# Turning the tables and the rows of a macaron S4D block by DMA transposes that read SBUF, without the copy in DRAM, and from the 16th group on

## The chip, the cores and the metric

The program runs on one core of one Trainium2 chip. The metric is the device time of one execution in microseconds; of the kernel before, three runs are given, and one further execution was profiled. Engines are named as the profile names them: PE (matrix products), PEld (its weight loads), DVE, ACT and POOL (the three engines for elementwise work) and SP, which only issues DMAs here.

## The reference

`x` has the shape (8, 2048, 256): 8 sequences, 2048 positions, 256 channels, float32. The output is

```python
x = x + 0.5 * ffn(layernorm(x))
x = x + attn(layernorm(x))       # an S4D convolution, then a layernorm
x = x + 0.5 * ffn(layernorm(x))

ffn(x)  = relu(x @ w1 + b1) @ w2 + b2            # 256 -> 1024 -> 256
attn(x) = layernorm(x + conv(x, K) + x * D) * ln_w + ln_b
K[h, l] = 2 * real(sum_n Ct[h, n] * exp(dtA[h, n] * l))     # 64 states n per channel h
```

The convolution is causal over all 2048 positions, one kernel `K` for each channel.

## The kernel before, in words

The work has three stages. **Stage a** is the first feed-forward sublayer, **the middle** is the S4D layer, **stage b** is the second feed-forward sublayer.

*The sublayers.* The 16384 tokens are cut into 64 groups of 256 (two sequences at 128 positions). The hidden width of 1024 is cut into eight slots of 128. In a slot, `up` (L848) makes six matmuls of 256 columns into a PSUM tile `ph` (a float32 product is made of three products of high and low parts, and there are two halves of the 256 channels), ACT takes the relu and DVE the low part (L926, L927: `hx`), and three slots later (`LAG`) `down` (L859) makes six matmuls into `po`. There are four `ph` banks and four `hx` buffers. PE needs the normalized tokens with the channels on the partitions: `xh` and `xl`, the high and low part of the transposed `xn`. They come in one of two ways, chosen in `ffn_in` (L752):

- *by PE*: four 128x128 transposes into `pt` (L794), then ACT's `xh` (L803) and DVE's `xl` (L805);
- *by DMA* (`turn_by_dma`, L810): DVE and ACT split `xn` into its two planes of 16-bit halves (`pl`, L815), SP writes them to a DRAM tile `xp` (L819), three slots later SP issues a DMA transpose from `xp` into `pt` (L823), three slots after that DVE and ACT put the halves together again (`xf`, L833, in an order fixed by hand), ACT makes `xh` (L835) and DVE `xl` (L837).

Stage a turns groups 0 to 43 by PE and 44 to 63 by DMA (`DMA_A = 44`), stage b groups 0 and 1 by PE and the rest by DMA (`DMA_B = 2`). `pre_a` and `pre_b` start the work on a group 18 or 19 slots before its first matmul.

*The tables P.* Beside stage a runs a background generator, `matrices` (L258): it makes, for every pair of channels (2 channels x 64 states on 128 partitions) the powers of the state's factor at 128 positions, real and imaginary. In 32 batches of four pairs, 128x1024 numbers each, `make` (L587) computes a batch on POOL into a room of `u` (there are four rooms, so batch n waits until batch n-4 has left), `spread` (L613) has ACT split it into planes of 16-bit halves (L620), SP writes these to DRAM (`pv`, L623) and the batch itself to `o_dram` (L625); `turn` (L628) issues a DMA transpose from `pv` back over `planes` (L631); `transpose` (L639) has DVE and ACT put the halves together in the batch's room (L646, order fixed by hand) and SP writes it to `pt_dram` (L650). There are two `planes` buffers, used in turn, and a batch goes through four steps of six sub-steps each (`BACK = 3`).

*What sets the order.* Each slot of stage a adds 1.32 to a clock; the generator names a price for each sub-step (9.1 or 10.3 for a batch, `PA` and `PB_`), and `fill` (L898) lets it run until it has caught up. Two marks are due: "half" at group 32 (the first 16 batches lie in a part of `u` that the output of groups 32 to 47 needs) and "tables" at group 48; what is missing then is emitted at once. SP, ACT and DVE run their instructions in the order of the program; the order itself is made by a scheduler, except where `keep_in_program_order` fixes it. All DMAs named here are issued by SP, except the loads `xa` (L981) and the stores `x_dram` (L999), which ACT issues.

*The middle* reads `pt_dram` and `o_dram`, runs the scan over 16 chunks on DVE and makes the outputs with PE. Nothing of it is changed.

Of the kernel before, what the change touches and what calls it, by code (L numbers as in the profile page):

```python
# [13 lines left out]
U16 = mybir.dt.uint16  # L14
# [5 lines left out]
P = 128  # L20
# [23 lines left out]
def macaron_s4d_kernel(  # L44
# [17 lines left out]
    nc = tc.nc  # L62
    V = nc.vector
    A_ = nc.scalar
# [3 lines left out]
    N = c_re.shape[1]  # L68
# [5 lines left out]
    NDC = H // P  # L74
    NFC = W // P
    NTB = 2
# [8 lines left out]
    PINT = 1  # L85
# [7 lines left out]
    BCH = 8  # L93
    NBT = H // BCH
# [6 lines left out]
    dram = ctx.enter_context(tc.tile_pool(name="dram", bufs=1, space=DRAM))  # L101
    ps = ctx.enter_context(tc.tile_pool(name="ps", bufs=2, space=PSUM))
    upool = ctx.enter_context(tc.tile_pool(name="upool", bufs=1))
    wpool = ctx.enter_context(tc.tile_pool(name="wpool", bufs=1))
# [4 lines left out]
    def bank(tag, name):  # L109
        return ps.tile([P, 512], F32, name=name, tag=tag, bufs=BANKS[tag])  # L110

    def slot(tag, shape, name, dtype=F32):
        return work.tile(shape, dtype, name=name, tag=tag, bufs=BUFS[tag])
# [99 lines left out]


    o_dram = [dram.tile([P, BCH * P], F32, name=f"o_{i}") for i in range(NBT)]
    pv_dram = [dram.tile([P, 2 * BCH * P], U16, name=f"pv_{i}") for i in range(2)]
    pt_dram = [dram.tile([P, BCH * P], F32, name=f"pt_{i}") for i in range(NBT)]
    kpad = dram.tile([H, KROW], F32, name="kpad")

# [38 lines left out]
    def matrices():  # L258
# [24 lines left out]
        for i, src in enumerate(raw + [dtx]):  # L283
            pt = bank("b", f"ptr{i}")
# [22 lines left out]
        r = zim  # L307
# [24 lines left out]
        f, a = r, z  # L332
# [133 lines left out]
        for i in range(H // P):  # L466
            nc.gpsimd.dma_start(
                out=kpad[i * P : (i + 1) * P, P + 1 :], in_=zeros[:, 0 : P - 1]
# [6 lines left out]
        with nc.allow_non_contiguous_dma(reason="256 numbers"):  # L475
            nc.gpsimd.dma_start(
                out=kpad.rearrange("(g c) k -> c g k", c=2)[:, :, P], in_=k0
# [100 lines left out]
        def p_of(bt):  # L578

            r, i = (room[2], 28 + bt % 4 * 8) if bt < first else (room[3], (16, 24, 48, 56)[bt % 4])  # L580
            return r[:, i * P : (i + 8) * P]
# [5 lines left out]
        def make(bt):  # L587

            E = G_
            pp = p_of(bt).rearrange("p (r g k) -> p r g k", r=2, g=PB)  # L590
            tm = tmp_of(bt)
            gs = slice(bt * PB, (bt + 1) * PB)
            br, bi = (
                pb[:, ri, gs, ::-1].unsqueeze(2).to_broadcast([P, PB, NA, NB]) for ri in range(2)
            )
            ar, ai = (
                pa[:, ri, gs, ::-1].unsqueeze(3).to_broadcast([P, PB, NA, NB]) for ri in range(2)
            )
            pr, pi = (pp[:, ri].rearrange("p g (a b) -> p g a b", b=NB) for ri in range(2))
            E.tensor_mul(pr, br, ar)  # L600
            yield
            E.tensor_mul(tm, bi, ai)
            yield
            E.tensor_sub(pr, pr, tm)
            yield
            E.tensor_mul(pi, br, ai)
            yield
            E.tensor_mul(tm, bi, ar)
            yield
            E.tensor_add(pi, pi, tm)  # L610
            yield

        def spread(bt):  # L613

            pl = planes[:, bt % 2]
            pu = p_of(bt).bitcast(U16).rearrange("p (m w) -> p w m", w=2)
            for _ in range(DI):
                yield
            for w in range(2):
                tc.keep_in_program_order(A_.copy(pl[:, w], pu[:, w]))  # L620
                yield
            via = pv_dram[bt % 2]
            nc.sync.dma_start(out=via, in_=pl.rearrange("p w m -> p (w m)"))  # L623
            yield
            nc.sync.dma_start(out=o_dram[bt], in_=p_of(bt))  # L625
            yield

        def turn(bt):  # L628
            for _ in range(PX):
                yield  # L630
            ins = nc.sync.dma_start(  # L631
                out=planes[:, bt % 2].rearrange("p w (k n) -> p (w k) n", n=P),
                in_=pv_dram[bt % 2], transpose=True,
            )
            if PINT:
                tc.keep_in_program_order(ins)
            yield

        def transpose(bt):  # L639
            pl, ptb = planes[:, bt % 2], p_of(bt)  # L640
            for _ in range(PY):
                yield
            pu = ptb.bitcast(U16).rearrange("p (c l r n w) -> p w r l c n", c=2, r=2, n=N, w=2)
            plv = pl.rearrange("p w (r l c n) -> p w r l c n", r=2, c=2, n=N)
            for w in range(2):
                ins = P_REINT[w](pu[:, w], plv[:, w])  # L646
                if PPIN:
                    tc.keep_in_program_order(ins)
            yield
            nc.sync.dma_start(out=pt_dram[bt], in_=ptb)  # L650
            yield

        planes = wpool.tile([P, 2, 2, BCH * P], U16, name="planes", tag="wE")
        P_REINT = (V.tensor_copy, A_.copy)
        PY = 0
        BACK = 3
        DI = 2
        PX = 2
        PA = 9.1
        PB_ = 10.3  # L660
        PPIN = 1

        beside = lags()
        for bt in range(NBT + BACK):
            parts = []
            if 0 <= bt - BACK < NBT:
                parts.append(transpose(bt - BACK))
            if 0 <= bt - 2 < NBT:
                parts.append(turn(bt - 2))
            if 0 <= bt - 1 < NBT:  # L670
                parts.append(spread(bt - 1))
            if bt < NBT:
                parts.append(make(bt))
            for n in range(6):
                for p in parts:
                    next(p, None)
                next(beside, None)
                yield (PA if bt < first + BACK else PB_) / 6
            if bt == first + BACK - 1:
                yield "half"  # L680
# [71 lines left out]
    def ffn_in(xt, name, on_act=NTB, by_dma=False, joint=None):  # L752
# [36 lines left out]
        if by_dma:  # L789
            return (yield from turn_by_dma(xn, name, Y2 - 1 if joint else Y2))  # L790
# [14 lines left out]
        V.tensor_sub(xl, ptv, xh.bitcast(F32))  # L805
        return xh, xl

    xp_dram = [dram.tile([P, 2 * NDC * NTB * P], U16, name=f"xp_{i}") for i in range(4)]

    def turn_by_dma(xn, name, y2):  # L810

        pl = slot("pl", [P, 2, NDC, NTB, P], f"pl_{name}", U16)
        xu = xn.bitcast(U16).rearrange("p i (d c w) -> p d i c w", d=NDC, w=2)
        for w, copy in DEINT:
            copy(pl[:, w], xu[:, :, :, :, w])  # L815
        yield
        via = xp_dram[turned_[0] % 4]
        turned_[0] += 1
        nc.sync.dma_start(out=via, in_=pl.rearrange("p w d i c -> p (w d i c)"))  # L819
        for _ in range(Y1):  # L820
            yield
        pt = slot("pl", [P, 2, NDC * NTB * P], f"pt_{name}", U16)
        nc.sync.dma_start(  # L823
            out=pt.rearrange("p w (k t) -> p (w k) t", t=P), in_=via, transpose=True
        )
        for _ in range(y2):
            yield
        xh = slot("xh", [P, NDC, TOK], f"xh_{name}", F32R)
        xl = slot("xl", [P, NDC, TOK], f"xl_{name}", F32R)
        xf = slot(XF, [P, NDC, TOK], f"xf_{name}")  # L830
        xv = xf.bitcast(U16).rearrange("p d (t w) -> p (d t) w", w=2)
        for w, copy in REINT:
            tc.keep_in_program_order(copy(xv[:, :, w], pt[:, w]))  # L833
        yield
        A_.copy(xh, xf)  # L835
        yield
        V.tensor_sub(xl, xf, xh.bitcast(F32))  # L837
        return xh, xl

    Y1, Y2 = 3, 3  # L840
    XF = "pl"
    DEINT = (0, V.tensor_copy), (1, A_.copy)
    REINT = (0, V.tensor_copy), (1, A_.copy)
    DMA_A = 44
    DMA_B = 2
    turned_ = [0]

    def up(wt, xT, ph, fc):  # L848
        xh, xl = xT
# [126 lines left out]
    def pre_a(g):  # L976
        by_dma = g >= DMA_A
        for _ in range(XL if g < JG else 0):
            yield
        xt = xts[g] = slot("x", [P, NTB, H], f"xa_{g}")  # L980
        ins = (nc.scalar if g >= JG else nc.sync).dma_start(out=xt, in_=hbm(x, g))  # L981
        if g >= JG:
            tc.keep_in_program_order(ins)
        for _ in range(XY):
            yield
        if g >= JG:
            joints[g - JG] = Joint(g - JG, by_dma)
        return (yield from ffn_in(xt, f"a{g}", NTB, by_dma, joints.get(g - JG)))
# [246 lines left out]
    def begin():  # L1235
        for _ in range(sizes[1] // PB):
            next(head)

    sublayer(
        w1t, w2t, pre_a, post_a, 18, "a", load_weights(), chain(matrices(), early()),  # L1240
        {"half": NG // 2, "tables": NG * 3 // 4},
        {NG * SLOTS - 6: lambda: next(head), NG * SLOTS - 1: begin},
# [127 lines left out]
```

## Time and profile before

| | |
|---|---|
| three runs | 1762.26, 1764.35, 1765.85 us; median 1764.35 |
| the profiled execution, its own time | 1761.45 us |
| its span in the trace | 1759.6 us |
| stage a, the middle, stage b (from the chain of work and the first and last products) | about 0 to 800, 800 to 1010, 1010 to 1760 us |
| DVE, ACT, POOL busy, share of the span | 78%, 56%, 33% |
| bytes moved by DMA | 242.68 MB, of them 206.36 MB from SP's queue |

A span is the time between the first and the last instruction that the trace shows; the execution's own time has 1.85 us more around it. A row of a view names the line, the engine, the operation, what is written and read, the count and times. In the views of waits, "A <- B" means that engine A stood idle and B's event ended that. Matmuls overlap in PE's pipeline, so the duration of one (270 to 290 ns) is longer than the distance at which they follow one another.

### The profile page before, as it was taken

To read this page: it belongs to the slowest core of one execution; us is meant where nothing else is said; L and a number is where in the kernel's file an instruction comes from. 1 tells how busy PE (TensorE), PEld (TensorE's weight loads), DVE (VectorE), ACT (ScalarE), POOL (GpSimd) and SP (SyncE) were. 2 spreads that over 40 slices of the span, in tenths; PEclk is the share of its full clock that TensorE was granted. 3 is DMA by queue.
4 is the path that set the end of the run, shared out by engine and by line. 5 is a ranking of instruction groups with operands and counts; after the bars stand their busy time and mean duration, and the time that the engine had idled before them with its cause. 6 is when DMAs were issued, how large, how long until landed. Compare 5 with 4: busy or idle time off the path is not lost.

```text
span 1759.6 us, 40994 instructions
## 1 busy us (share of the span) xinstructions
PE 1724.2 (98%) x15367; PEld 1697.3 (96%) x15367; DVE 1373.7 (78%) x4405; ACT 986.3 (56%) x2178; POOL 588.7 (33%) x550
## 2 busy tenths in 40 slices
PE   9999999989999999999999799999999999999998
PEld 7999999989999999999999799999999999999998
DVE  6998877767776667766999788888888888888884
ACT  4555467667777755544555445555555555555553
POOL 1117989875775115111000122222222222222220
PEclk9999999999999999999999999999999999999999
DMA  5111177669768633246888913333333333333331
GB/s 189 49 37 52 48 214 227 215 185 269 246 218 243 167 101 99 91 111 197 265 261 261 277 55 91 97 91 95 89 94 91 95 92 95 86 97 91 95 92 49
DMA packets 293277, 242.68 MB, mean 138 GB/s; under 512 B 164564, under 2 KB 237012, under 8 KB 292566
## 3 DMA queue, kind: packets, MB, share of 16 engines
q1 hardware_dynamic: 265648, 206.36, 41.1%
q10 hardware_dynamic: 26502, 32.52, 5.4%
q8 instruction: 120, 1.97, 0.4%
q0 software_dynamic: 928, 1.19, 0.3%
q14 instruction: 79, 0.65, 0.1%
HBM read 91.89 MB, written 109.84 MB: 115 GB/s over the span
## 4 chain that ended last, share of the span: by engine, by line
PE 64%; DVE 10%; DMA 3%; issue 1%; ACT 1%; POOL 0%; SPq 0%; ACTq 0%; DVEq 0%; POOLq 0%
PE ph_b L854 21%; PE po_b L864 21%; PE po_a L864 10%; PE ph_a L854 10%; DVE e L1127 2%; DVE te L1128 2%; DMA planes<-pv 1%; DVE xsB L1130 1%; DVE xsA L1130 1%; DVE xsA L1129 1%; DVE xsB L1129 1%; PE py L1172 1%; DVE xsE L1130 0%; DMA pt_a<-xp 0%; DMA xp<-pl_a 0%
## 5 line engine op out<-in xcount | busy, mean ns | idle before, releaser
L864 PE MATMUL po_a<-wa,hx_a 128*128 128x256 f32 x3072 | 456.7, 285 | 11.4 <-DVE hx_a L116 11.2
L854 PE MATMUL ph_a<-xh_a,wa 128*128 128x256 f32 x2048 | 457.0, 287 | 0.8 <-ACT xh_a L803 0.7
L854 PE MATMUL ph_b<-xh_b,wb 128*128 128x256 f32 x2048 | 442.8, 284 | 0.7 <-ACT xh_b L803 0.7
L864 PE MATMUL po_b<-wb,hx_b 128*128 128x256 f32 x3072 | 441.4, 283 | 2.0 <-DVE hx_b L116 2.0
L864 PEld LDWEIGHTS po_a<-wa,hx_a 128*128 128x128 f32 x3072 | 407.2, 192 | 13.8 <-DVE hx_a L116 13.1
L864 PEld LDWEIGHTS po_b<-wb,hx_b 128*128 128x128 f32 x3072 | 400.5, 192 | 2.4 <-DVE hx_b L116 2.4
L854 PEld LDWEIGHTS ph_a<-xh_a,wa 128*128 128x128 f32 x2048 | 356.4, 193 | 3.6 <-ACT wa L194 1.5
L854 PEld LDWEIGHTS ph_b<-xh_b,wb 128*128 128x128 f32 x2048 | 353.0, 193 | 1.1 <-ACT xh_b L803 1.1
L926 ACT ACTIVATE hx_b<-ph_b 128x256 fp32r<-128x256 f32 x512 | 192.0, 381 | 241.5 <-PE ph_b L854 222.9
L926 ACT ACTIVATE hx_a<-ph_a 128x256 fp32r<-128x256 f32 x512 | 194.9, 387 | 236.0 <-PE ph_a L854 222.0
L116 DVE SCALAR_TENSOR_TENSOR hx_a<-ph_a,hx_a 128x256 fp32r<-128x256 f32 x512 | 209.8, 414 | 125.5 <-ACT hx_a L926 123.2
L854 PE MATMUL ph_a<-xl_a,wa 128*128 128x256 f32 x1024 | 290.7, 285 | 0.0
L854 PE MATMUL ph_b<-xl_b,wb 128*128 128x256 f32 x1024 | 285.3, 284 | 0.0
L1305 POOL TENSOR_TENSOR xb<-xb,lnb_sb 128x512 f32<-128x512 f32 x64 | 82.6, 1292 | 504.8 <-DMA xb<-x_dram 342.4
L116 DVE SCALAR_TENSOR_TENSOR hx_b<-ph_b,hx_b 128x256 fp32r<-128x256 f32 x512 | 210.3, 414 | 52.3 <-ACT hx_b L926 46.3
L854 PEld LDWEIGHTS ph_a<-xl_a,wa 128*128 128x128 f32 x1024 | 198.0, 193 | 0.8 <-DVE xl_a L805 0.4
L854 PEld LDWEIGHTS ph_b<-xl_b,wb 128*128 128x128 f32 x1024 | 197.7, 193 | 0.0
L777 POOL TENSOR_TENSOR xa<-xa,hb 128x512 f32<-128x512 f32 x64 | 88.6, 1384 | 282.2 <-ACT xn L730 252.0
L777 POOL TENSOR_TENSOR xb<-xb,hb 128x512 f32<-128x512 f32 x64 | 95.1, 1486 | 55.2 <-ACT xn L730 23.5
L730 ACT ACTIVATE xn<-xb,nb_fb,t_fb 128x255 f32<-128x255 f32 x127 | 69.5, 594 | 76.4 <-DVE nb_fb L116 76.4
L815 DVE COPY pl_b<-xn 128x512 uint16<-128x512 uint16 x62 | 44.5, 717 | 73.3 <-ACT xn L730 73.3
L730 ACT ACTIVATE u<-xa,nb_u,t_u 128x256 f32<-128x256 f32 x104 | 90.1, 866 | 0.0
(263 smaller groups left out, 2511.9 us busy)
## 6 DMA issues: line engine op xcount, KB each, us to landing
o<-u SPq DMA_DIRECT2D x32, 512.0 KB, 3.4
pv<-planes SPq DMA_DIRECT2D x32, 512.0 KB, 3.6
pt<-u SPq DMA_DIRECT2D x32, 512.0 KB, 3.7
tz<-kpad SPq DMA_DIRECT2D x64, 256.0 KB, 4.7
xb<-x_dram SPq DMA_DIRECT2D x64, 256.0 KB, 2.7
out_dram<-xb SPq DMA_DIRECT2D x64, 256.0 KB, 2.9
x_dram<-xa ACTq DMA_DIRECT2D x62, 256.0 KB, 2.0
xp<-pl_b SPq DMA_DIRECT2D x62, 256.0 KB, 2.0
```

The source lines that it names most:

```text
L116: return V.scalar_tensor_tensor(out=o, in0=a, scalar=s, in1=b, op0=op0, op1=op1)
L730: ins = A_.activation(dst, src, AF.Identity, bias=nb[:, i : i + 1], scale=rs[:, i : i + 1])
L777: return G_.tensor_add(xt, xt, hb2.unsqueeze(1).to_broadcast([P, NTB, H]))
L815: copy(pl[:, w], xu[:, :, :, :, w])
L854: nc.tensor.matmul(ph, wt[wp][:, dc, fs], xp[:, dc, :], start=(n == 0), stop=(n == 3 * NDC - 1))
L864: nc.tensor.matmul(po[:, i, :], hp[:, tsl], wt[wp][:, fc, :], start=(fc == 0 and i == 0 and n == 0), stop=(fc == NFC - 1 and n == 2), skip ...
L926: last[A_] = A_.activation(hh, ph, AF.Relu)
L1127: E.tensor_mul(t1, xv[:, :, :, j, :], wr_b)
L1128: E.tensor_mul(t2, xv[:, ::-1, :, j, :], wi_b)
L1129: E.tensor_add(xv[:, :, :, j + 1, :], xv[:, :, :, j + 1, :], t1)
L1130: E.tensor_add(xv[:, :, :, j + 1, :], xv[:, :, :, j + 1, :], t2)
L1305: G_.tensor_add(xt, xt, lnb_sb.unsqueeze(1).to_broadcast([P, NTB, H]))
```

## The change

The DRAM tiles `pv` and `xp` go. The DMA transposes read the planes where they lie in SBUF. For P the two `planes` buffers become one for the planes and one, `turned`, for the transposed planes; a batch goes through three steps (`BACK = 2`), ACT's two copies of a batch, SP's transpose and the putting together have an order fixed by hand, and the putting together starts at the fifth sub-step. For the rows, six slots lie between the issue of the transpose and the putting together, as the two times three did. `DMA_A` goes from 44 to 16, so groups 16 to 43 of stage a change from PE to DMA. Stage b keeps its choice.

```diff
     o_dram = [dram.tile([P, BCH * P], F32, name=f"o_{i}") for i in range(NBT)]
-    pv_dram = [dram.tile([P, 2 * BCH * P], U16, name=f"pv_{i}") for i in range(2)]
...
         def spread(bt):
 
-            pl = planes[:, bt % 2]
             pu = p_of(bt).bitcast(U16).rearrange("p (m w) -> p w m", w=2)
-            for _ in range(DI):
+            yield
+            yield
+            for w in range(2):
+                tc.keep_in_program_order(A_.copy(planes[:, w], pu[:, w]))
                 yield
-            for w in range(2):
-                tc.keep_in_program_order(A_.copy(pl[:, w], pu[:, w]))
-                yield
-            via = pv_dram[bt % 2]
-            nc.sync.dma_start(out=via, in_=pl.rearrange("p w m -> p (w m)"))
+            tc.keep_in_program_order(nc.sync.dma_start(
+                out=turned.rearrange("p w (k n) -> p (w k) n", n=P),
+                in_=planes.rearrange("p w m -> p (w m)"), transpose=True,
+            ))
             yield
             nc.sync.dma_start(out=o_dram[bt], in_=p_of(bt))
             yield
 
-        def turn(bt):
-            for _ in range(PX):
-                yield
-            ins = nc.sync.dma_start(
-                out=planes[:, bt % 2].rearrange("p w (k n) -> p (w k) n", n=P),
-                in_=pv_dram[bt % 2], transpose=True,
-            )
-            if PINT:
-                tc.keep_in_program_order(ins)
-            yield
-
         def transpose(bt):
-            pl, ptb = planes[:, bt % 2], p_of(bt)
-            for _ in range(PY):
+            ptb = p_of(bt)
+            for _ in range(4):
                 yield
             pu = ptb.bitcast(U16).rearrange("p (c l r n w) -> p w r l c n", c=2, r=2, n=N, w=2)
-            plv = pl.rearrange("p w (r l c n) -> p w r l c n", r=2, c=2, n=N)
+            plv = turned.rearrange("p w (r l c n) -> p w r l c n", r=2, c=2, n=N)
             for w in range(2):
-                ins = P_REINT[w](pu[:, w], plv[:, w])
-                if PPIN:
-                    tc.keep_in_program_order(ins)
+                tc.keep_in_program_order(P_REINT[w](pu[:, w], plv[:, w]))
             yield
             nc.sync.dma_start(out=pt_dram[bt], in_=ptb)
             yield
 
-        planes = wpool.tile([P, 2, 2, BCH * P], U16, name="planes", tag="wE")
+        both = wpool.tile([P, 2, 2, BCH * P], U16, name="planes", tag="wE")
+        planes, turned = both[:, 0], both[:, 1]
         P_REINT = (V.tensor_copy, A_.copy)
-        PY = 0
-        BACK = 3
-        DI = 2
-        PX = 2
+        BACK = 2
...
         for w, copy in DEINT:
             copy(pl[:, w], xu[:, :, :, :, w])
         yield
-        via = xp_dram[turned_[0] % 4]
-        turned_[0] += 1
-        nc.sync.dma_start(out=via, in_=pl.rearrange("p w d i c -> p (w d i c)"))
-        for _ in range(Y1):
-            yield
         pt = slot("pl", [P, 2, NDC * NTB * P], f"pt_{name}", U16)
         nc.sync.dma_start(
-            out=pt.rearrange("p w (k t) -> p (w k) t", t=P), in_=via, transpose=True
+            out=pt.rearrange("p w (k t) -> p (w k) t", t=P), in_=pl.rearrange("p w d i c -> p (w d i c)"),
+            transpose=True,
         )
         for _ in range(y2):
             yield
...
-    Y1, Y2 = 3, 3
+    Y2 = 6
...
-    DMA_A = 44
+    DMA_A = 16
     DMA_B = 2
```

More of the change, by code (lines that the diff above doesn't have):

```diff
@@ L651, in transpose @@
             yield
-        planes = wpool.tile([P, 2, 2, BCH * P], U16, name="planes", tag="wE")
+        both = wpool.tile([P, 2, 2, BCH * P], U16, name="planes", tag="wE")
+        planes, turned = both[:, 0], both[:, 1]
         P_REINT = (V.tensor_copy, A_.copy)
-        PY = 0
-        BACK = 3
-        DI = 2
-        PX = 2
+        BACK = 2
         PA = 9.1
         PB_ = 10.3
-        PPIN = 1
         beside = lags()
@@ L667, in matrices @@
                 parts.append(transpose(bt - BACK))
-            if 0 <= bt - 2 < NBT:
-                parts.append(turn(bt - 2))
             if 0 <= bt - 1 < NBT:
@@ L806, in ffn_in @@
         return xh, xl
-    xp_dram = [dram.tile([P, 2 * NDC * NTB * P], U16, name=f"xp_{i}") for i in range(4)]
     def turn_by_dma(xn, name, y2):
@@ L843, in macaron_s4d_kernel @@
     REINT = (0, V.tensor_copy), (1, A_.copy)
-    DMA_A = 44
+    DMA_A = 16
     DMA_B = 2
-    turned_ = [0]
     def up(wt, xT, ph, fc):
```

## The prediction

> **What bounds the kernel now.** First the page's busy times, then its chain of the work that ended last:
>
> ```profile
> PE 1724.2 (98%) x15367; PEld 1697.3 (96%) x15367; DVE 1373.7 (78%) x4405; ACT 986.3 (56%) x2178; POOL 588.7 (33%) x550
> ...
> PE 64%; DVE 10%; DMA 3%; issue 1%; ACT 1%; POOL 0%; SPq 0%; ACTq 0%; DVEq 0%; POOLq 0%
> ```
>
> PE is full, so what is taken from PE comes off the time unless another engine cannot follow. Where that could be, the busy times by stretch tell (us, PE, PEld, DVE, ACT, POOL, then granted clock, DMA share, GB/s):
>
> ```profile
> 224.00:340.00 116.00, 115.47 (x970) 115.07 (x969) 86.90 (x222) 80.23 (x155) 102.44 (x104) 1.00 0.72 215
> 340.00:425.00 85.00, 77.13 (x616) 76.73 (x615) 59.34 (x148) 59.32 (x112) 60.85 (x54) 0.94 0.83 233
> 425.00:450.00 25.00, 24.77 (x208) 24.57 (x207) 18.86 (x55) 20.03 (x38) 17.68 (x15) 1.00 0.82 246
> 450.00:550.00 100.00, 100.00 (x840) 100.00 (x839) 72.15 (x205) 74.64 (x144) 72.64 (x62) 1.00 0.74 233
> 550.00:600.00 50.00, 47.31 (x389) 46.60 (x389) 31.79 (x102) 37.26 (x74) 12.01 (x10) 1.00 0.82 218
> ```
>
> These five stretches are the batches of P. From 450 to 550 PE never stops; between 340 and 425 it stands still for 7.9 us and its granted clock falls to 0.94, between 550 and 600 for 2.7. The waits from 224 to 600 name who was late:
>
> ```profile
> ACT u L646 <- DMA planes<-pv: 18.1, 8, 7.0
> DVE u L646 <- DMA planes<-pv: 12.9, 6, 6.5
> PEld po_a L864 <- DVE hx_a L116: 12.5, 7, 5.0
> ```
>
> ACT and DVE stand in the copies that put a batch of P together, for the DMA transpose; the relus queue behind those copies, and PE waits for the relus' `hx`. The worst is at 387: the transpose needs 9.56 us to land, and PE loses 4.8.
>
> **What the change takes from PE.** The timeline of PE around one group's four transposes:
>
> ```profile
> 506.74 0.64 PE L864 MATMUL po_a<-wa,hx_a 128*128 128x256 f32 x4
> 507.22 0.27 PE L794 MATMUL pt_a<-ident,xn 128*128 128x128 f32 x1
> 507.25 0.48 PE L864 MATMUL po_a<-wa,hx_a 128*128 128x256 f32 x2
> 507.57 0.28 PE L854 MATMUL ph_a<-xh_a,wa 128*128 128x256 f32 x1
> 507.69 0.28 PE L854 MATMUL ph_a<-xl_a,wa 128*128 128x256 f32 x1
> 507.81 0.49 PE L794 MATMUL pt_a<-ident,xn 128*128 128x128 f32 x3
> 508.05 0.48 PE L854 MATMUL ph_a<-xh_a,wa 128*128 128x256 f32 x2
> 508.37 0.28 PE L854 MATMUL ph_a<-xl_a,wa 128*128 128x256 f32 x1
> ```
>
> Products of 256 columns start 0.12 us apart. From 506.74 to 508.37 are 1.63 us with ten of them, 1.20 us; the four transposes take the other 0.43. The groups say the same: the additions of `po` (line 992) of groups 33 to 41 run from 448.14 to 543.66, eight periods of 11.94 us; groups that DMA turns, in the chain from 600.02 to 623.06, follow at 11.52. So 0.42 us a group, and 28 groups (16 to 43) change: 28 x 0.42 = **11.8 us off the path**, as long as PE stays the bound.
>
> **What comes on in its place.** Each of the 28 groups gets the copies of the DMA way, by the medians of the 20 groups that go it already: on ACT a plane (L815) 0.61, the putting together (L833) 0.77, and `xh` 0.62 for 0.59, together 1.41 us; on DVE 0.43, 0.46, and `xl` 0.69 for 0.67, together 0.91. From 450 to 550 ACT is busy 74.64 of 100, 8.91 us a group; with the new copies 10.3 of 11.52, 90%. DVE goes from 8.61 to 9.5, 83%. So both still fit beside PE, and I cost them at nothing; the cover is ACT's last 1.2 us a group, and if jitter eats it, the price is the gain, up to 11.8. On SP each group adds a transpose of 1.24 us (L823). SP loses the 32 + 82 plain writes and the waits for their landing (line 823 waited 101.4 us in stage b and 34.5 in stage a for `xp`), so it is no fuller. There a row's transpose can stand behind one of P, which holds SP 3.1 us (median of L631), and behind `pt`, which waits for the putting together; the 3.1 and the 3.4 us to landing fit into the six slots, 8.6 us, that the order leaves, and what exceeds them is a wait of ACT in `xf`, part of rival A.
>
> **P.** A batch goes through one DMA less: `pv` took 3.6 us from issue to landing, 32 times 0.5 MB, 16 MB of 242.68; the rows' `xp` takes out 82 times 0.25 MB, 20 MB. In the stretch 340 to 425, with the DMA engines 83% busy, that is the relief where PE stood still. Against it: in the changed program's order of ACT, batches 5 to 15 are put together only three or four relus after the copies (before, five to nine), three relus being 4.3 us at 1.44 each; the transpose, now fixed on SP, takes 4.4 / 6.0 / 8.2 us (least, median, most) to land. ACT will then wait 1 to 2 us in about ten batches. PE bears that: `down` is three slots, 4.3 us, behind `up`, of which relu and low part need 0.8. From batch 16 on more than a group, over 11 us, lies between, and nothing waits. The single `turned` buffer makes a cycle of transpose 6.0, putting together 1.4 and SP's issue: about 8 us, under the 9.1 / 1.32 x 1.44 = 9.9 us at which the batches are let out. I put relief and tightness against each other at 0 for 340 to 425, with ends of -13 (7.9 of standing still and 6% of 85 us by the clock all gone) and +12 (ten batches at 1.2, the gain lost).
>
> Between 560 and 582 the chain runs through SP and `xp`: SP's line 631 holds 3.99, `xp` lands in 3.46, `pt_a` in 4.11. Both DRAM copies go; of the 2.7 us that PE stands there I take 1 off (ends 0 and -2.7).
>
> **Stage b** is PE's at 11.52 a group, and nothing on PE changes. Its third group, the first by DMA, has the chain `xp` (issued 1030.71), `pt_b` (1034.20, 3.44 us), and PE stands 2.1 us at 1037; without `xp`'s 3.5 us that goes: -2.1 (ends 0 and -2.1).
>
> **The unknown.** No row of before shows a transpose whose source is in SBUF. Bounds by the nearest rows: as the transpose from DRAM (6.0 and 3.4 us to landing), or less by what the DRAM read costs, at most the 2.0 us of a whole `xp` write; upward, the 9.56 us of the worst transpose. I take the row as it is. A group in stage b has 8.6 us (six slots) between issue and use, so there even 8 us are hidden.
>
> [...]
>
> **The sum.** 1761.45 - 11.8 - 2.1 - 1 + 0 = 1746.5 us against the profiled execution. That one was 2.9 us under the median of the three runs, 1764.35; on the median's scale the forecast is **1749**.
>
> **Rivals.**
> *A, ACT takes PE's place.* The order puts six row turns and eight batches into groups 26 to 31, where ACT had 59.32 of 85 us busy already; with 1.41 us for each of the seven groups there that is 69 of 85, 82%, plus the waits of 1 to 2 us. For: it is ACT and DVE that stood in the waits shown. Against: 450 to 550 ran without a stop. It gives the 11.8 back and leaves stage b's gain: 1759 to 1768, around 1762.
> *B, the slower side: the transpose from SBUF is slow, and ACT waits for it with the relus behind.* The place is batches 0 to 15 (225 to 425 us). ACT comes to the putting together 4.3 us after the copies, PE has 3.5 in hand; so it decides from a landing of about 8 us on. At 9.56, 1.8 us in each of 12 batches, 21 us against 15 gained: 1770; at 12 us, 50: 1800.
> *C, the P stretch heals.* With `pv` gone the transposes land in time and the 13 us of 340 to 425 go too: 1736. For: in the critical chain there, 16 of 85 us are two transposes beside `pv`, `o` and `pt`. Against: less distance to the putting together.
> *D, nothing of it shows.* It cannot be, unless A holds: PE's transposes are on the path of every group that changes.
>
> **How the numbers follow.** Forecast (1741 to 1758) 0.48, C (1732 to 1741) 0.15, A 0.17, B 0.20. A measurement of this kernel tells 0.2%, 3.5 us, from no change, so "same" is 1760.8 to 1767.9. Faster: 0.48 + 0.15 + 0.05 of A = 0.68; same: the most of A, 0.10; slower: B and A's end, 0.22. The range runs from C's 1736 to B's middle, 1785; the forecast's own is 1741 to 1758.
>
> **What would show it.** Right: no line 794 for groups 16 to 43, periods of 11.52 between 450 and 543 with PE never stopped, ACT near 90% there; `turned` landing in 4 to 7 us. Wrong: PE waiting for `hx` in long pieces behind ACT's putting together (line 635 of the new kernel), landings over 8 us, ACT's waits for the rows' `pt_a`, or SP held for more than 3 us by a row transpose.

## The result, and the profile after

The changed kernel takes 1790.83 us (median of four runs, 1785.7 to 1798.69) where the kernel before takes 1764.41: **1.0151 times as long, 95% interval 1.0118 to 1.0184**, 26.6 us slower. The forecast was 1749, faster, with a range from 1736 to 1785; the time lies above it. The profiled execution took 1798.69 us, the slowest of the four, with a span of 1796.9: it is 37.3 us longer than the profiled execution before, so what the traces show as lost is more than the 26.6 us of the medians.

The page of the changed kernel, its busy times and its chain by engine:

```profile
PE 1727.7 (96%) x15255; PEld 1694.5 (94%) x15255; DVE 1419.1 (79%) x4461; ACT 1015.7 (57%) x2234; POOL 600.9 (33%) x550
...
PE 78%; DVE 10%; DMA 7%; ACT 2%; issue 1%; ACTq 0%; DVEq 0%; SPq 0%
```

PE has its 112 transposes less, but no less busy time (1727.7 us after 1724.2): after a stop of 6.6 us that ends at 329.18 its next products start 0.21 us apart instead of 0.12, and the granted clock is down to 0.91 between 340 and 450. It is also idle for more of a longer span. The stretches of P (us; PE, PEld, DVE, ACT, POOL; granted clock, DMA share, GB/s):

```profile
224.00:340.00 116.00, 101.85 (x804) 98.80 (x803) 88.61 (x211) 78.49 (x151) 94.01 (x95) 0.97 0.63 166
340.00:425.00 85.00, 68.10 (x529) 66.53 (x528) 65.32 (x146) 58.95 (x107) 64.97 (x56) 0.91 0.65 184
425.00:450.00 25.00, 23.90 (x182) 23.70 (x182) 16.36 (x46) 20.19 (x38) 10.90 (x9) 0.91 0.89 228
450.00:550.00 100.00, 89.73 (x719) 88.05 (x719) 70.34 (x194) 74.65 (x142) 65.46 (x54) 0.98 0.68 174
550.00:600.00 50.00, 46.14 (x378) 45.32 (x377) 37.89 (x101) 39.83 (x77) 34.15 (x29) 1.00 0.75 190
```

PE stops in every one, also from 450 to 550, where it never did before. The whole loss lies there, as the times between DVE's additions of `po` (line 967; 992 before) show, in the two profiled executions (us, from the addition of the first group named to the addition of the group after the last):

| groups | 16 to 24 | 25 to 32 | 33 to 43 | 44 to 49 | 50 to 61 | group 62 to stage b | stage b |
|---|---|---|---|---|---|---|---|
| before | 115.8 | 107.6 | 133.9 | 71.7 | 144.8 | 213.6 | 747.5 |
| after | 130.4 | 123.7 | 141.0 | 70.6 | 144.8 | 216.0 | 745.3 |

The transposes themselves did what was hoped of them. The view of line 620, P's transpose from SBUF:

```profile
L620 SPq DMA_TRANSPOSE planes<-planes x32: 1317/2085/3899, 225.5 to 624.0; - x32
...
DMA to landing us min/median/max: 4.2/4.5/7.2
```

It lands after 4.5 us (6.0 from DRAM) and holds SP 2.1 (3.1). The rows' land after 3.1 us (3.4). The waits from 224 to 620 name others:

```profile
DVE st_fa L675 <- DMA xa<-in_L_attn_x_dram: 44.0, 19, 5.0
DVE hx_a L116 <- ACT hx_a L901: 36.9, 43, 4.1
PEld po_a L839 <- DVE hx_a L116: 32.9, 25, 4.8
...
ACT u L635 <- DMA planes<-planes: 9.2, 6, 2.6
ACT planes L618 <- DMA planes<-planes: 6.8, 5, 2.4
```

DVE now stands 44 us at the statistics of a group for its load of `x` (14.8 before, from 224 to 600), and ACT's wait for the transpose has halved (9.2 after 18.1). PE waits for `hx` 25 times instead of 7. Three places show how DVE falls behind. The first, DVE's and then POOL's timeline around 322:

```profile
320.48 0.68 DVE L967 TENSOR_TENSOR xa<-po_a,xa 128x512 f32<-128x512 f32 x1
321.71 4.02 DVE L795 COPY pl_a<-xn 128x512 uint16<-128x512 uint16 x1 [0.56 <-ACT xn L712]
325.65 1.58 DVE L635 COPY u<-planes 128x1024 uint16<-128x1024 uint16 x1
```

```profile
321.13 1.07 POOL L599 TENSOR_TENSOR u<-u 128x512 f32<-128x512 f32 x1
322.15 1.06 POOL L605 TENSOR_TENSOR u<-u 128x512 f32<-128x512 f32 x1
323.16 1.05 POOL L607 TENSOR_TENSOR u<-u 128x512 f32<-128x512 f32 x1
324.17 1.26 POOL L759 TENSOR_TENSOR xa<-xa,hb 128x512 f32<-128x512 f32 x1
325.40 1.23 POOL L607 TENSOR_TENSOR u<-u 128x512 f32<-128x512 f32 x1
```

A row copy of 0.43 us takes 4.02: it stands while four of POOL's instructions follow one another without a gap, and ends 0.3 us after the fourth. Behind it DVE makes a copy of a batch and the statistics before it comes to the next low part of a relu, and PE stands 6.6 us. The second stands in the chain of work at 366:

```profile
366.75 5.59 DVE nb_u L116
```

This is a step of a group's statistics that both kernels have; it takes 0.16 us where POOL is idle, and this one takes 5.67 beside five of POOL's instructions in a row; PE stands 4.6 us behind it. So it is not only the added copies that stand beside POOL. The third, DVE and then ACT around 472:

```profile
472.43 0.42 DVE L116 SCALAR_TENSOR_TENSOR hx_a<-ph_a,hx_a 128x256 fp32r<-128x256 f32 x1
477.85 0.75 DVE L675 BATCH_NORM_STATS2 st_fa<-xa 128x6 f32<-128x256 f32 x2 [5.01 <-DMA xa<-in_L_attn_x_dram]
```

```profile
470.84 0.39 ACTq L956 DMA_DIRECT2D xa<-in_L_attn_x_dram  x1
```

ACT issues the load at 470.84, and it lands 7.0 us later (2.8 in the median of these loads). Under way beside it are a transpose (issued at 468.32, landed 4.4 us later), `pt` (from 470.49) and `o` (at 471.43, landed 7.8 us later); how much each of them delays it is not shown. DVE stands 5.0 us with the low parts of the relus behind it.

### The profile page after: what moved, and what is told of

The parts are those of the page before. It is cut to its first block, busy times and chain, and to the rows that moved or that the text cites. A ratio compares the mean times of both kernels' runs of the same rounds, so it can differ in the third digit from the quotient of the medians.

```text
span 1796.9 us, 40484 instructions
## 1 busy us (share of the span) xinstructions
PE 1727.7 (96%) x15255; PEld 1694.5 (94%) x15255; DVE 1419.1 (79%) x4461; ACT 1015.7 (57%) x2234; POOL 600.9 (33%) x550
## 4 chain that ended last, share of the span: by engine, by line
PE 78%; DVE 10%; DMA 7%; ACT 2%; issue 1%; ACTq 0%; DVEq 0%; SPq 0%
PE ph_b L829 21%; PE po_b L839 21%; PE po_a L839 13%; PE ph_a L829 13%; DMA xa<-in_L_attn_x_dram 4%; PE py L1138 3%; PE py L1147 3%; PE pv L1072 3%; DVE hx_a L116 2%; DVE q_u L116 2%; DMA planes<-planes 1%; DVE u L635 1%; DVE st_fa L675 1%; DVE xf_a L809 1%; ACT planes L618 1%
## 5 line engine op out<-in xcount | busy, mean ns | idle before, releaser
L759 POOL TENSOR_TENSOR xa<-xa,hb 128x512 f32<-128x512 f32 x64 | 92.7, 1449 | 312.3 <-ACT xn L712 281.4
L675 DVE BATCH_NORM_STATS2 st_fa<-xa 128x6 f32<-128x256 f32 x128 | 48.2, 417 | 58.7 <-DMA xa<-in_L_attn_x_dram 58.5
L795 DVE COPY pl_b<-xn 128x512 uint16<-128x512 uint16 x62 | 34.0, 548 | 74.1 <-ACT xn L712 74.1
```

The source lines that it names most:

```text
L675: ins = V.bn_stats(st[:, i, :], src)
L759: return G_.tensor_add(xt, xt, hb2.unsqueeze(1).to_broadcast([P, NTB, H]))
```

## The experiments

Beside each run the kernel before was timed on the same chip (its median was 1764 to 1770 us on different occasions), so the ratios are compared; differences in us are the ratio times 1764.4.

| run | ratio, 95% interval | us against before |
|---|---|---|
| changed kernel | 1.0151 (1.0118 to 1.0184) | +26.6 |
| 1 P new, rows by DMA from 44 | 1.0025 (1.0012 to 1.0038) | +4.4 |
| 2 kernel before, rows from 16, through DRAM | 1.0177 (1.0157 to 1.0196) | +31.2 |
| 3 P old, rows from SBUF from 16 | 1.0095 (1.0072 to 1.0117) | +16.8 |
| 4 changed, x two slots earlier | 1.0135 (1.0112 to 1.0157) | +23.8 |
| 5 changed, POOL light | 0.9937 (0.9918 to 0.9957) | -11.1 |
| 6 before, POOL light | 0.9926 (0.9911 to 0.9941) | -13.1 |
| 7 P old, rows from SBUF from 44 | 0.9962 (0.9948 to 0.9975) | -6.7 |
| 8 as 7, from 33, x early | 1.0052 (1.0035 to 1.0069) | +9.2 |
| 9 as 5, x early | 1.0005 (0.9987 to 1.0023) | +0.9 |
| 10 as 1, two buffers for P | 0.9976 (0.9959 to 0.9993) | -4.2 |
| 11 changed, row copies on ACT | 1.0127 (1.0089 to 1.0165) | +22.4 |
| 12 changed, two buffers for P | 1.0080 (1.0063 to 1.0098) | +14.1 |
| 13 as 11, x early | 1.0091 (1.0072 to 1.0109) | +16.1 |
| 14 as 7, from 33 | 0.9990 (0.9980 to 1.0000) | -1.8 |

### Which part costs: runs 1, 2, 3 and 7

```diff
# run 1, on the changed kernel
-    DMA_A = 16
+    DMA_A = 44
# run 2, on the kernel before
-    DMA_A = 44
+    DMA_A = 16
# run 3, on the kernel before (run 7: the same with DMA_A left at 44)
-        nc.sync.dma_start(out=via, in_=pl.rearrange("p w d i c -> p (w d i c)"))
...
-            out=pt.rearrange("p w (k t) -> p (w k) t", t=P), in_=via, transpose=True
+            out=pt.rearrange("p w (k t) -> p (w k) t", t=P), in_=pl.rearrange("p w d i c -> p (w d i c)"),
+            transpose=True,
...
-    DMA_A = 44
+    DMA_A = 16
```

> The changed kernel with groups 16 to 43 turned by PE again; P and stage b keep the transposes that read SBUF. Theory R (the added row work of the 28 groups on DVE and ACT is what costs): the loss of 26 us goes with it, 1755 to 1764 us. Theory P (the batches of P, put together sooner after their copies and with a single buffer for the transposed planes, hold ACT and DVE): the loss stays and PE's 11.8 us come back on top, 1795 to 1805. Theory S (transposes that read SBUF disturb the other transfers, the loads of x above all): between, 1770 to 1790, since the 32 transposes of P remain beside the loads.

> The kernel before, with the copies in DRAM, but groups 16 to 63 of stage a turned by DMA. Theory R: slow as the changed kernel or slower, 1785 to 1810. Theories P and S: neither of their causes is here, so PE's gain of 11.8 us shows: 1750 to 1760.

> P as in the kernel before (two buffers, copy in DRAM, four steps), the rows as in the changed kernel (from SBUF, from the 16th group on). Theory R: 1780 to 1800. Theory P: the gain shows, 1748 to 1758. Theory S: some of the loss, 1765 to 1785.

> P as before, in stage a the same groups by DMA as before (44 to 63), and only the rows' copy in DRAM left out. What the source in SBUF is worth by itself for the rows: the stop of 2.1 us at the start of stage b and part of the 2.7 us around 575 go: 2 to 4 us faster than before. If the difference of the first run of this study (rows from 44, P new: 4 us slower than before) is P's new order, this one must lie about 6 to 8 us under that one; if it is the transposes from SBUF themselves, as slow as that one.

Runs 1 and 2 speak for theory R: without the 28 groups' rows the loss falls to 4.4 us (1769 on the scale of 1764, where theory R had at most 1764), and with both copies in DRAM the 28 groups cost even more, 31.2. Run 3, 1781 on the scale of 1764, lies within the ranges of R and of S. Theory S falls with run 7, which takes out the rows' DRAM copy alone and is 6.7 us *faster* than before (2 to 4 were expected), and because the 28 groups are dearer through DRAM than from SBUF (run 2 against run 3). Taken from run 7, P new costs 11.1 us (run 1 less run 7), the 28 groups 23.5 with P old (run 3 less run 7) and 22.2 with P new (changed less run 1): within the intervals the two parts are independent, and together they make the change, -6.7 + 11.1 + 22.2 = 26.6. If PE's gain of 11.8 is in the 22.2, the rows brought an estimated 34 us of standing.

### P's part: runs 10 and 12

```diff
+        def pair(bt):
+            if bt < first:
+                return both[:, bt % 2], more[:, bt % 2]
+            return both[:, 0], both[:, 1]
...
+        more = room[3][:, 48 * P : 64 * P].bitcast(U16).rearrange("p (i w m) -> p i w m", i=2, w=2)
```

> The first run of this study (P new, rows by DMA from group 44) with two buffers for the planes and two for the transposed planes in the first 16 batches, in free cells of the fourth room of u. That run was 11 us slower than the one with P old. Theory B (the single buffers: ACT stands 16 us before it may split the next batch, DVE and ACT put together under the transpose's eyes): 4 to 10 us come back, 1757 to 1763 on the scale of 1764. Theory O (the short distance of three relus between the copies and the putting together, which stays): as that run, about 1768.

> The changed kernel (rows from the 16th group) with the two buffers each for planes and transposed planes in the first 16 batches. If the price of the single buffers (8.6 us, from the two runs with rows from 44) and that of the rows are independent: 26.6 - 8.6 = 18 us slower than before, 1782 on the scale of 1764. If the rows' loss is only there because the single buffers make P late: level with before or faster, 1752 to 1764.

Two buffers give back 8.6 us with the rows from 44 (run 1 to run 10; theory B had 4 to 10) and 12.5 with the rows from 16 (changed to run 12; 1778 where independent prices gave 1782). So most of P's 11.1 is the single buffers, and it is a loss of its own; run 10, whose P transposes read SBUF too, is faster than before. In the traces of runs 1 and 10 it lies in groups 16 to 32, beside the batches that have two buffers: 16 to 24 take 119.4 us instead of 123.1, 25 to 32 take 107.4 instead of 112.6, and 33 to 43 take 135.3 in both. ACT's wait before it may split the next batch, from 224 to 620, of run 1 and then of run 10:

```profile
ACT planes L618 <- DMA planes<-planes: 16.3, 12, 3.2
```

```profile
ACT planes L624 <- DMA planes<-planes: 7.8, 6, 2.4
```

Up to 405 us, where run 10 has its second buffers, this wait is 5.2 us in run 1 and nothing in run 10; the rest of it lies where both have one. Which waits make up the other part of the 8.6 us is not shown.

### The rows' part: POOL, the load of x, and where DVE's copies are made

```diff
# runs 5, 6 and 9
             E.tensor_mul(pr, br, ar)
             yield
-            E.tensor_mul(tm, bi, ai)
             yield
-            E.tensor_sub(pr, pr, tm)
             yield
             E.tensor_mul(pi, br, ai)
             yield
-            E.tensor_mul(tm, bi, ar)
             yield
-            E.tensor_add(pi, pi, tm)
             yield
# runs 4, 8, 9 and 13
-    XY = 4
+    XY = 6
-        w1t, w2t, pre_a, post_a, 18, "a", load_weights(), chain(matrices(), early()),
+        w1t, w2t, pre_a, post_a, 20, "a", load_weights(), chain(matrices(), early()),
# runs 11 and 13
+        on_act = name[0] == "a" and int(name[1:]) < 44
...
-            copy(pl[:, w], xu[:, :, :, :, w])
+            (A_.copy if on_act else copy)(pl[:, w], xu[:, :, :, :, w])
...
-            tc.keep_in_program_order(copy(xv[:, :, w], pt[:, w]))
+            tc.keep_in_program_order((A_.copy if on_act else copy)(xv[:, :, w], pt[:, w]))
...
-                last[A_] = A_.activation(hh, ph, AF.Relu)
+                if tag == "a" and 16 <= g < 44 and fc in (1, 5):
+                    last[A_] = V.tensor_scalar_max(hh, ph, 0.0)
+                else:
+                    last[A_] = A_.activation(hh, ph, AF.Relu)
# run 14, on run 7 (run 8: with x early too)
-    DMA_A = 44
+    DMA_A = 33
```

> The changed kernel with two of POOL's six products and sums for a batch of P, so that P is wrong (it leaves out the products of the imaginary factor) and POOL has a third of that work. Theory C (DVE's added copies, all of them SBUF to SBUF, stand until POOL's run of work on P ends, and that is what slows the 28 groups): most of the loss goes, about 1750 to 1760 on the scale of 1764, and the median of DVE's copies returns to 0.43 and 0.46 us in the 28 groups. Theory D (ACT and DVE simply have too much to do in order, or the transfers are late): 1775 to 1790.

> The control for the run above: the kernel before with the same two of six operations of POOL (P wrong in the same way). Theory C: it gains less than the changed kernel does, down to about 1750 to 1758, and the changed kernel is then level or up to 12 us ahead of it, instead of 26 behind. Theory D: both gain alike and the 26 us between them stay.

"POOL light" means that POOL makes two of its six products and sums for a batch of P and leaves out those with the imaginary factor. With POOL light in both, the changed kernel is 2 us behind the kernel before, instead of 26.6: the loss needs POOL's work beside it. In the 28 groups the median of DVE's copy that puts a row together falls from 0.86 us to 0.45, and all of DVE's row copies there from 44 us to 30. Run 5 alone does not tell the stand of DVE's copies from batches that POOL simply delivers sooner. PE in the first half of P, 224 to 425, of the changed kernel and then of run 5:

```profile
224.00:425.00 201.00, 169.95 (x1331) 165.33 (x1330) 153.93 (x356) 137.44 (x257) 158.98 (x150) 0.94 0.64 174
```

```profile
224.00:425.00 201.00, 189.70 (x1525) 186.20 (x1524) 140.86 (x406) 158.62 (x297) 78.46 (x82) 0.98 0.76 190
```

More is done in the same time (1525 products instead of 1331), with DVE busy for less. But theory C had 12 us ahead as its best, and run 5 is level. The groups say why: 33 to 43 take 127.8 us in run 5 and 132.7 in run 6, where PE turns them, so there the rows gain 4.9 us, about the 11 times 0.42 of the prediction; 16 to 32 take 223.9 instead of 210.7, and these 13.2 us are lost even with POOL light.

> The changed kernel; stage a starts a group 20 slots ahead instead of 18 and loads x six slots before its statistics instead of four, so the load has 2.9 us more. Theory X (within R: DVE stands 44 us, from 224 to 620, at the statistics of a group because the load of x is issued by ACT too late for its landing of up to 7 us, and PE with it): most of those waits go, 1755 to 1770. Theory C (within R: DVE's added copies stretch beside POOL's work on P, as the 4.0 us of one copy of 0.43, and DVE is simply too slow): little change, 1780 to 1790.

Over the whole kernel theory X misses: 2.8 us come back, inside the intervals. By groups it holds for one stretch. The earlier lead costs 5 us up to group 16; groups 33 to 43 take 130.9 instead of 141.0, and PE hardly stops from 450 to 550 of run 4 (89.73 in the changed kernel), with 8.0 us of DVE's waits for `xa` left of 44.0:

```profile
450.00:550.00 100.00, 98.81 (x811) 97.58 (x810) 85.27 (x219) 85.22 (x162) 70.73 (x57) 1.00 0.82 207
```

> The changed kernel with POOL's work on P cut to two of six operations (P wrong, as in the two light runs before) and x loaded two slots earlier, at the price of 3 to 4 us at the start that the earlier lead of two slots showed. If DVE's stand beside POOL and DVE's stand for the load of x are the two causes and there is no third, nothing keeps the 28 groups from 11.52 us plus the other products: about 12 us less than the light version of the kernel before (1753) and 4 for the start, 1743 to 1748. If a third cause holds them, it stays at 1750 to 1757.

It is 12 us slower than run 5, at 1765 on the scale of 1764, so both cases of this expectation failed: the two cures do not add up. The earlier lead costs 4.8 us up to group 16, and groups 16 to 43 take 358.5 us instead of 351.7 although DVE's waits for `xa` in them fall from 47.6 to 22.3. The largest wait of ACT for a DMA is the single buffer (21.0 us in 12 waits for `planes`), but run 5 has nearly the same (18.7). Why run 9 is slower stays open.

> The changed kernel; in groups 16 to 43 ACT makes both row copies of DVE, and DVE two of the eight relus, which it reads from PSUM, so that DVE's added copies between SBUF buffers are gone and ACT has 0.6 us a group more. Theory C (DVE's copies beside POOL): a third to a half of the loss comes back, 1772 to 1782 on the scale of 1764. If ACT's place in the order is what costs, it gets worse: 1795 to 1810.

> The changed kernel with both cures at once: the row copies of groups 16 to 43 off DVE (ACT makes them, DVE takes two relus of eight from PSUM) and x loaded two slots earlier. Theory C plus X (DVE stands beside POOL in the first half of P and for the load of x in the second): groups 25 to 32 stay at 106 to 108 us as with the copies on ACT alone, groups 33 to 43 fall from 139 to about 131; 1770 to 1780 on the scale of 1764, the stop of 16 us in groups 16 to 24 gone or not. If either loss stays where it was, its cause is another.

On the scale of 1764 run 11 lies at 1787, between its two cases, and run 13 at 1780, the upper end of its range. The stretches tell more (us). Each row is one execution, and the changed kernel's took 7.9 us more than its median, the others at most 4.6 more; differences of a few us between rows are not shown.

| groups | 16 to 24 | 25 to 32 | 16 to 32 | 33 to 43 |
|---|---|---|---|---|
| changed | 130.4 | 123.7 | 254.1 | 141.0 |
| run 4, x early | 132.5 | 118.4 | 250.9 | 130.9 |
| run 11, copies on ACT | 143.4 | 106.4 | 249.8 | 138.7 |
| run 13, both | 140.5 | 104.5 | 245.0 | 133.5 |
| run 12, two buffers | 124.1 | 113.0 | 237.1 | 138.6 |
| run 3, rows from 16, P old | 133.7 | 120.3 | 254.0 | 131.4 |
| run 7, no rows here, P old | 119.6 | 108.7 | 228.3 | 130.4 |

In groups 25 to 32 the time with the row copies off DVE is that of run 7 (106.4 and 104.5). But the border after group 24 flatters this: in the changed kernel the period of group 23 is 29.0 us and that of 24 only 6.2, and over 16 to 32 together the copies off DVE bring back 4.3 us (run 11) and, beyond x early, 5.9 (run 13), of the 25.8 that lie above run 7; two buffers bring back 17.0. So that DVE's row copies make the whole loss there is not shown. In 33 to 43 it is the load of `x`: the two rows with x early take 130.9 and 133.5, the three without 138.6 to 141.0. With P old (run 3) these groups lose nothing without any earlier load, and DVE waits 13 us for `xa` in the 28 groups instead of 44; so this wait is made by the rows and the new P together. With POOL light (run 5) DVE waits as long, 47.6 us, and the groups still take 127.8; that fits a wait that costs only where DVE has no time to spare. Groups 16 to 24 hold in both runs 11 and 13 one long stop of ACT, which stands in a copy of `planes` for POOL's batch; ACT's timeline of run 11:

```profile
332.77 1.04 ACT L618 COPY planes<-u 128x1024 uint16<-128x1024 uint16 x1 [14.71 <-POOL u L609]
```

What makes the rows dear in groups 16 to 24 therefore stays open: POOL light brings them to 123.0 and two buffers to 124.1, but no run separates the causes there.

> As the run before this, but groups 33 to 43 by DMA too, where POOL is a third less busy than in the first half of P, and x loaded two slots earlier. If the loss of the rows is made in the first half of P alone, the 11 groups gain 11 times 0.42, 4.6 us: 6 to 8 us faster than before. If any group beside P loses: slower than the run before this by 5 us or more.

> P as before, rows from SBUF and by DMA from group 33, x as early as before (without the two slots of the run from 33 with x early, which was 9 us slower than before). If the groups 33 to 43 are harmless and the earlier lead was that run's loss: 4 to 8 us faster than before, near the run from 44 (6.7 faster). If the groups cost as such: level or slower.

Run 14 lies between its two cases, 4.9 us behind run 7. So even in the second half of P, 11 more groups cost 4.9 us instead of bringing 4.6. The other 11 us of run 8 came with the earlier lead. With P old there is hardly a wait for it to cure (DVE's waits for `xa` from 224 to 620 are 10.8 us in run 14); why the lead costs as much as 11 us is not shown.

## Why the prediction was wrong

- *"Both still fit beside PE, and I cost them at nothing."* This is the step that failed: the overlap of the 28 groups' row work with PE was taken for free, and it cost 22 to 23.5 us net. Two sizes in it were wrong. First, DVE's row copies went in with 0.43 and 0.46 us, the medians of groups 44 and later, most of which come when POOL has finished P. Of the 96 row copies of DVE in the changed kernel's trace of stage a, the 37 that start while an instruction of POOL is running have a median of 1.06 us and take up to 4.02, the other 59 have 0.43. In the time of the 28 groups the copies take 44 us instead of 25. Second, DVE's 8.61 us a group were those of 450 to 550. By the prediction's own rows DVE is busier in the first half of P: from the addition of group 16 to that of 31 it is busy 146.0 us for 15 groups, 9.7 each, before, and 170.9, 11.4 each, in the changed kernel, where 9.5 were forecast and PE needs 11.52. Over all 28 groups it is busy 292.6 us, 10.45 each, and stands 1.6 more for `xa`: 12.0. A group takes 14.1 there, so this sum names the engine that is late and does not add up to the whole loss.
- *The price of the failure, "up to 11.8".* Wrong by a factor of three: an estimated 34 us of standing came on (22.2 and the 11.8 that they used up). Rival A saw the place (the engines behind PE), named ACT rather than DVE, and thought the loss ended where PE's gain was used up. At 322 a stand of 4.0 us in one copy of DVE is a stop of 6.6 us for PE, and PE's granted clock is 0.91 from 340 to 450.
- *P: relief against tightness, 0 with ends of -13 and +12.* 11.1, near the upper end. The mechanism named, ACT and DVE waiting for the landing, was not most of it: run 10 keeps the short distance and leaves 2.5 us of the 11.1, and ACT's wait there is 9.2 us in the changed kernel after 18.1. The single buffers, which the text had dismissed as a cycle of 8 us within 9.9, were: 8.6 to 12.5 us.
- *Rival B, a slow transpose from SBUF.* That 1790.83 lies between its 1770 and 1800 is luck: the landings were shorter, 7.2 us at most for P, and its condition of about 8 us was never met.
- *PE's 11.8 us.* The size of the gain was right: in run 5 groups 34 to 36 follow at 11.53, 11.52 and 11.52 us, in its control, run 6, at 11.95, 11.93 and 11.94. No run shows the whole 11.8; in runs 2, 3 and 14 it was outweighed.
- *Stage b's start, -2.1, and the SP chain around 575, -1.* Right: PE's idle time for `hx_b` goes from 2.0 to 0.0, stage b from 747.5 to 745.3, and groups 41 to 45 take 58.5 us in run 7 after 61.5. Run 7, which has these and nothing else, is 6.7 us faster, more than the 3.1 foreseen.

## What to carry to other kernels

Price an added instruction from rows of the stretch in which it will run, with the same neighbours at work, not from the same instruction elsewhere (here DVE's row copies had a median of 1.06 us beside POOL and 0.43 without); and count for an engine that works in order its waits as well as its busy time (here 44 us of DVE's for `xa`). Take a change of several parts apart: here leaving out the rows' DRAM copy alone (run 7) beats both kernels, 0.9962 (0.9948 to 0.9975), while the parts built on top of it lose. The transfer saved for P did not pay here when the second buffer went with it: P cost 11.1 us (run 1 against run 7), and 2.5 with two buffers in its first half (run 10 against run 7).

## What the runs showed of the hardware

- In the changed kernel's trace of stage a, DVE's copies of rows between SBUF buffers take longer beside POOL, and not only to the end of the instruction in progress: 0.43 us in the median where POOL is idle at their start, 1.06 where it works, and 4.02 in one copy through four of POOL's instructions of 1.05 to 1.26 us without gaps. The small steps of the statistics from SBUF (128x4, line 116) do too: 0.16 us in the median where POOL is idle, up to 5.67 beside it. The relus' low parts, which read PSUM, and the first step of the statistics (line 675) take 0.41 to 0.42 us in the median with and without POOL. What in the chip makes the one kind stand and the other not is not shown.
- In these two traces the DMA transpose from SBUF is no dearer than from DRAM: 1.25 us on SP for a row transpose of stage a (1.24 from DRAM), 2.1 for P's (3.1), landings of 3.1 (3.4) and 4.5 (6.0) us, the latter with the DMA engines less busy than before (0.65 instead of 0.83 from 340 to 425).
